# Masked attention with a residual on one core: the context matmuls of a pair of heads issued in one group instead of three

## The chip, the cores and the metric

The kernel runs on one core of a Trainium2 chip. A core has a matrix engine (TensorE, PE in the profile, with its weight loads as PEld), a vector engine (VectorE, DVE), an activation engine (ScalarE, ACT), a general engine (GpSimd, POOL) and an engine that issues transfers (SyncE, SP), all fed by instruction queues of their own and synchronised by semaphores. PE writes its results to PSUM; everything else lies in SBUF, 128 partitions wide both. The metric is the time of one execution on the device in microseconds.

## The reference

```python
def _L0_cond_ref(x, mask, Wq, Wo):          # x: (16, 512, 1024), mask: (16, 1024) of 0 and 1
    NH = 8
    B, D, T = x.shape
    dk = D // NH                            # 64
    scale = 1.0 / jnp.sqrt(dk)
    xt = jnp.transpose(x, (0, 2, 1))
    q = xt @ Wq.T
    qh = q.reshape(B, T, NH, dk).transpose(0, 2, 1, 3)
    scores = scale * jnp.einsum('bhqd,bhkd->bhqk', qh, qh)
    cmask = mask[:, None, None, :]
    rmask = mask[:, None, :, None]
    logits = (scores * cmask + (1.0 - cmask) * NEG) * rmask
    attn = jax.nn.softmax(logits, axis=-1)
    ctx = jnp.einsum('bhqk,bhkd->bhqd', attn, qh)
    ctx = ctx.transpose(0, 2, 1, 3).reshape(B, T, D)
    out = ctx @ Wo.T
    return jnp.transpose(out, (0, 2, 1))
x = x + _L0_cond_ref(x, cond_2048, L0_cond_Wq, L0_cond_Wo)
```

Queries, keys and values are one projection. A token whose mask is 0 is no key for the others, and its own row of logits is all zero, so its attention is the plain mean over all tokens.

## The kernel before

About half of the 1024 tokens of a batch element count. The kernel gathers those (up to C = 544 of them) into dense *slots*: four blocks of 128 slots and a *tail* of 32. Attention is computed among the slots alone. The others get the mean, which is projected once for a group of three or four batch elements and added to their rows.

The 16 batch elements go through a software pipeline. While element b has its scores and context computed, the next one, n = b + 1, has its rows transposed (`xt`, L398), projected to queries (`query`, L421) and transposed to values (`value`, L467), and the one before, o = b - 1, has its context normalised (`norm`, L664 to L670) and projected out (`project`, L680), added to the residual (L685) and scattered to the output (L764).

The attention of an element runs in 18 *steps*, the list `S` in `run`. A step is (p, i): pair of heads p (0 to 3) and slot block i (0 to 3); two more steps (p, None), after (0, 1) and after (2, 3), do the tails of four heads at once. In a step PE computes two score tiles (`scores`, L580: 4 matmuls of 128x272 for each head, in float16 with the low halves added by a second matmul), and ACT takes the exponential of each into a tile `p` of 128x544 in SBUF (L584), with the sums of the rows. The score tiles `pss` have two buffers. A tail step has 16 small matmuls (L555), one exponential (L559), a split into high and low parts on DVE (L564, L565) and four transfers by SP that spread them into `pt` (L571, L572).

The *context* of a pair is accumulated in one PSUM tile `pav`, which has one buffer. `attend(b, p, i, ps)` adds slot block i: 4 matmuls, L597, whose stationary operand is 128x64, so that the two heads of a pair write to partitions 0 to 63 and 64 to 127. They are in float32, and the profile counts each twice: 1024 in the program, 2048 in the trace. `attend(..., 4, None)` adds the tail with 4 matmuls of 128x128 (L600), and then ACT copies `pav` into an SBUF tile `c` (L604). `c` has three buffers, `p` has nine.

What `run` emits in a step, in order: the work that waits for this step (`free[st]`: sums of rows for the means, the reciprocals of the row sums in `recip_sums` and `recip_rows`, `norm`), the scores of both heads, one indirect transfer from the POOL queue (`issue`), and then a share of the *fill*, the list `m` of pieces of work for the elements n and o. Each piece has a cost in us, written out by hand, and the fill is dealt out so that after step st a share (st + 1) / 18 of the total has been emitted.

The context is emitted with the fill. `todo` gathers the `attend` calls of blocks 0 to 3 and `ready` holds those that are due. The blocks of steps 0 and 1 go out as one group in step 3, those of steps 2 and 3 as one group in step 1 of the next pair, and the tail, held in `whole`, goes out in step 2 of the next pair, between the scores of its two heads, with the copy of `pav` behind it:

```python
now = []
if i in (0, 2):
    ready, todo = todo, []
elif i in (1, 3):
    now, ready = ready, []
for f in fill + now if big else now + fill:
    f()
if i is not None:
    todo.append(L(self.attend, b, p, i, ps))
if i == 3:
    (whole if p < 3 else todo).append(L(self.attend, b, p, 4, None))
```

For the last pair of an element the tail goes with blocks 2 and 3, in step 1 of the next element.

The order emitted is not the order run. A list scheduler puts the instructions of all engines in order by their priority (the place where they were emitted, with an offset for some) and by when it holds their inputs and buffers to be ready, so it may put other work of PE into a group or split one.

The reciprocals of a pair: `recip_sums` (L619 to L627, DVE) two steps after its last block, `recip_rows` three steps after: a transpose on PE (L633, called *rr* here), a copy (L636), and SP transfers out to DRAM (L638) and back, broadcast (L641), for `norm`.

[...]

Of the kernel before, what the change touches and what calls it, by code (L numbers as in the profile page):

```python
# [10 lines left out]
F32 = mybir.dt.float32  # L11
# [8 lines left out]
P = 128  # L20
# [10 lines left out]
C = 544  # L31
CT = C - 512
CH = C // 2
# [16 lines left out]
class Fast:  # L50
# [491 lines left out]
    def scores(self, b, p, i):  # L542


        nc, s = self.nc, self.st[b]
        if "z" not in s:
            s["z"] = self.sb([P, H, 4], F32, "z", 2)
            s["zt"] = self.sb([P, 2], F32, "zt", 2)
        if i is None:
            pt = self.ps_s.tile([P, 2, 512], F32, tag="s", name="pss")  # L550
            for a in range(2):
                for g in range(2):
                    for r in range(HG):
                        xx, k = s["xx"][2 * p + r // 2], r % 2
                        self.beat = nc.tensor.matmul(pt[r * CT:(r + 1) * CT, g, :CH], lhsT=xx[:, 2 * k, 512:C],  # L555
                                                     rhs=xx[:, 2 * k + a, g * CH:(g + 1) * CH],
                                                     start=(a == 0), stop=(a == 1)).ins
            t = self.sb([P, C], F32, "p", 9)
            nc.scalar.activation(t.rearrange("p (g c) -> p g c", g=2), pt[:, :, :CH], AF.Exp,  # L559
                                 bias=s["nm"][p][:, HG:], scale=SCALE, accum_out=s["zt"][:, p:p + 1])  # L560

            hi = self.sb([P, C], F32R, "c", 3)
            lo = t.bitcast(F32R)
            nc.vector.tensor_copy(hi, t)  # L564
            nc.vector.tensor_tensor(lo, t, hi.bitcast(F32), ALU.subtract)  # L565

            def spread():
                s["pt"] = self.sb([P, 2, C], F32R, "pt")
                half = slice(0, DK), slice(DK, P)
                for k in range(2):  # L570
                    nc.sync.dma_start(out=s["pt"][half[k], k, :].bitcast(F32), in_=hi[half[k]].bitcast(F32))  # L571
                    nc.sync.dma_start(out=s["pt"][half[1 - k], k, :].bitcast(F32), in_=lo[half[k]].bitcast(F32))  # L572

            self.later(spread)
            return None
        xx, k = s["xx"][p // 2], p % 2
        pt = self.ps_s.tile([P, 2, 512], F32, tag="s", name="pss")
        for a in range(2):
            for g in range(2):
                self.beat = nc.tensor.matmul(pt[:, g, :CH], lhsT=xx[:, 2 * k, i * P:(i + 1) * P],  # L580
                                             rhs=xx[:, 2 * k + a, g * CH:(g + 1) * CH],
                                             start=(a == 0), stop=(a == 1)).ins
        t = self.sb([P, C], F32, "p", 9)
        self.exp = [nc.scalar.activation(t.rearrange("p (g c) -> p g c", g=2), pt[:, :, :CH], AF.Exp,  # L584
                                         bias=s["nm"][p // HG][:, p % HG:p % HG + 1], scale=SCALE,
                                         accum_out=s["z"][:, p, i:i + 1]).ins]
        return t

    def attend(self, b, p, i, ps):
        nc, s = self.nc, self.st[b]  # L590
        if i == 0:
            s["pav"] = self.ps_av.tile([P, 2, 512], F32, tag="av", name="pav")
        for g in range(2):
            for k in range(2):
                cols = slice(g * CH, (g + 1) * CH)
                if i < 4:
                    nc.tensor.matmul(s["pav"][k * DK:(k + 1) * DK, g, :CH], lhsT=s["v"][p][:, i, k * DK:(k + 1) * DK],  # L597
                                     rhs=ps[k][:, cols], start=(i == 0), stop=False)
                else:
                    nc.tensor.matmul(s["pav"][:, g, :CH], lhsT=s["vt"][p // 2][:, k, p % 2 * 2:p % 2 * 2 + 2, :],  # L600
                                     rhs=s["pt"][:, p % 2, cols], start=False, stop=(k == 1))
        if i == 4:
            c = self.sb([P, C], F32, "c", 3)
            nc.scalar.copy(c.rearrange("p (g c) -> p g c", g=2), s["pav"][:, :, :CH])  # L604
            s["c"].append(c)


    def recip(self, b, p):
# [191 lines left out]
    def run(self, flag):  # L800
        B = self.B
        L = lambda f, *a: lambda: f(*a)
        S = [(p, i) for p in range(NP) for i in range(4)]
        S.insert(2, (0, None))
        S.insert(13, (1, None))
        N = len(S)

        def xt(n):
            return [(0.45, L(self.xt, n, c)) for c in range(4)] + [(0.25, L(self.xt, n, 4))]

# [14 lines left out]
        for i, e in enumerate(ends):  # L825
            g = list(range(ends[i - 1] + 1 if i else 0, e + 1))
# [33 lines left out]
        def shift0():  # L860
            with self.tc.high_priority(offset=HPO):
                self.shift(0, 0)

        first = query(0, 0, 0) + xt(0)[3:] + [(0, L(self.facts, 0, 2))] + query(0, 1, 0) + query(0, 0, 1)
        first += [(0, index1)] + value(0, 0) + g1[:1] + query(0, 1, 1)[:1] + g1[1:2]
        first += [(0, L(self.split, "q", c, 1)) for c in range(DC)]
# [11 lines left out]
        begin += [(0, L(self.load, "o", c)) for c in range(DC)]  # L878
        begin += [(0, L(self.range_x, 0, c)) for c in range(DC)] + [(0, L(self.range_w, "q"))]
        groups = [(g, min(h, B)) for g, h in ((2, 4), (4, 8), (8, 12), (12, 16)) if g < B]  # L880
        todo, ready, whole = [], [], []
        for b in range(B + 1):
            o, n = b - 1, b + 1
            if b == B:
                self.last(o, todo)
                break
            free, early, late = {}, ([], []), []
            if b >= 1:
# [56 lines left out]
            total = sum(c for c, _ in m)  # L945
            done, pos = 0.0, 0
            for st, (p, i) in enumerate(S):
                soon, self.soon = self.soon, []
                for f in soon + free.get(st, []):
                    f()  # L950
                if i is None:
                    self.scores(b, p, None)
                else:
                    ps = [self.scores(b, 2 * p, i)]
                    if i == 2 and whole:
                        whole.pop()()
                    ps.append(self.scores(b, 2 * p + 1, i))

                for _ in range(1 if b < B - 2 else -(-len(self.urgent + self.spare) // (N - st))):
                    self.issue()  # L960
                goal = total * (st + 1) / N
                fill = []
                while pos < len(m) and (done + m[pos][0] / 2 <= goal or st == N - 1):
                    fill.append(m[pos])
                    done += m[pos][0]
                    pos += 1

                big = st >= 4 and [c >= 1 for c, _ in fill if c > 0.1][:1] == [True]
                fill = [f for _, f in fill]

                now = []
                if i in (0, 2):
                    ready, todo = todo, []
                elif i in (1, 3):
                    now, ready = ready, []
                for f in fill + now if big else now + fill:
                    f()
                if i is not None:
                    todo.append(L(self.attend, b, p, i, ps))
                if i == 3:  # L980
                    (whole if p < 3 else todo).append(L(self.attend, b, p, 4, None))
                    if p < 3:
                        free.setdefault(st + 2, []).append(L(self.recip_sums, b, p))
                        free.setdefault(st + 3, []).append(L(self.recip_rows, b, p))
                        if p < 2 or b == B - 1:
                            free.setdefault(st + 5, []).append(L(self.norm, b, p))
# [136 lines left out]


# [10 lines left out]
```

## Time and profile before

| | |
|---|---|
| four runs | 1133.4, 1133.7, 1134.68, 1137.15 us, median 1134.19 |
| the profiled execution | 1131.44 us, its span 1129.7 us |
| granted PE clock over it | 0.995 |
| ACT: exponentials L584 | 512, 363.3 us busy, 714 ns each |
| ACT: copy of the context L604 | 64, 38.7 us busy, 604 ns each |
| PE: scores L580 | 2048, 302.8 us busy |
| PE: context L597 and its tail L600 | 2048 and 256, 296.2 and 48.7 us busy |
| PE: queries L421 | 1536 of 128x272 or 128x274 |
| PE: output projection L680 | 852 in the program, of 128x512 for the most part |
| POOL: gathers and scatters L313, L764 | 284, about 1 us each |

Busy time is the union of an instruction group's records; matmuls are pipelined, so that each lasts longer than the distance to the next one. What a matmul costs is therefore read from the distances between starts, not from its length.

### The profile page before, as it was taken

How to read it: one execution, taken by the hardware profiler on the slowest of the kernel's cores; microseconds unless marked ns; L12 is line 12 of the kernel's file. 1: busy time of each engine (PE TensorE's matmuls, PEld its weight loads, DVE VectorE, ACT ScalarE, POOL GpSimd, SP SyncE). 2: the span in 40 equal slices, each digit the busy share in tenths (PEclk: the TensorE clock that was granted, in tenths of full speed). 3: DMA queues.
4: the chain of work that ended last, by engine and by line, in shares of the span. 5: the costliest groups of instructions: out<-in, count | busy, mean ns of one | idle time of the engine just before them, and what ended most of it. 6: DMA issues, size and time to landing. Idle time of an engine off the chain costs nothing.

```text
span 1129.7 us, 23296 instructions
## 1 busy us (share of the span) xinstructions
PE 1088.2 (96%) x8386; PEld 706.5 (63%) x8386; DVE 731.9 (65%) x2369; ACT 676.1 (60%) x1716; POOL 286.7 (25%) x303
## 2 busy tenths in 40 slices
PE   7899999999999999999999999999999999998997
PEld 6566666666666666566666666566666666665553
DVE  7687566765665667667665766856566665665643
ACT  5776665666566666566565665666656566654540
POOL 3001031322202222222222222232222222214542
PEclk9899999999999999999999999999999999999999
DMA  7745455645545464655655566455665654545652
GB/s 237 205 117 148 135 163 146 190 129 180 146 125 176 126 203 139 173 172 160 187 151 169 153 180 184 123 180 145 195 166 150 190 150 135 149 124 172 203 163 85
DMA packets 78122, 181.35 MB, mean 161 GB/s; under 512 B 15008, under 2 KB 16800, under 8 KB 78000
## 3 DMA queue, kind: packets, MB, share of 16 engines
q1 hardware_dynamic: 56816, 111.62, 36.0%
q0 software_dynamic: 21184, 68.18, 18.6%
q8 instruction: 68, 1.11, 0.4%
q14 instruction: 54, 0.44, 0.1%
HBM read 92.34 MB, written 33.91 MB: 112 GB/s over the span
## 4 chain that ended last, share of the span: by engine, by line
PE 68%; DVE 12%; DMA 9%; issue 6%; ACT 2%; POOL 2%; SPq 0%; DVEq 0%; POOLq 0%; ACTq 0%
PE pav L597 19%; PE pss L580 16%; PE pm L680 13%; PE pm L421 9%; PE pm L398 3%; DMA xi<-x_in,idx 2%; PE pav L600 2%; DMA rb<-rd 2%; PE pm L467 2%; POOL y_out L764 2%; DMA rd<-rr 1%; PE pm L633 1%; DVE c L664 1%; ACT p L584 1%; DMA xm<-x_nat_in 1%
## 5 line engine op out<-in xcount | busy, mean ns | idle before, releaser
L584 ACT ACTIVATE p<-pss,nm 128x544 f32<-128x544 f32 x512 | 363.3, 714 | 230.8 <-PE pss L580 219.3
L580 PE MATMUL pss<-xx 128*128 128x272 f16 x2048 | 302.8, 281 | 4.3 <-DMA xx<-hl 2.5
L597 PE MATMUL pav<-p,v 128*64 128x272 f32 x2048 | 296.2, 401 | 0.9 <-ACT c L604 0.9
L580 PEld LDWEIGHTS <-xx 128*128 128x128 f16 x2048 | 192.0, 99 | 85.4 <-issue 40.9
L597 PEld LDWEIGHTS pav<-p,v 128*64 128x64 f32 x2048 | 140.2, 136 | 104.6 <-issue 40.0
L764 POOL DMA_INDIRECT y_out<-xa,idx x68 | 68.3, 1005 | 304.1 <-PE pss L580 163.0
L421 PE MATMUL pm<-xh,wqh 128*128 128x274 f16 (+1 forms) x512 | 143.8, 281 | 0.1
L421 PE MATMUL pm<-xl,wqh 128*128 128x274 f16 (+1 forms) x512 | 143.3, 280 | 0.2 <-DVE xl L359 0.2
L421 PE MATMUL pm<-xh,wql 128*128 128x274 f16 (+1 forms) x512 | 143.4, 280 | 0.0
L313 POOL DMA_INDIRECT xa<-x_in,idx x68 | 70.3, 1034 | 182.4 <-PE pss L580 89.3
L421 PEld LDWEIGHTS <-wqh 128*128 128x128 f16 x1024 | 99.9, 99 | 22.0 <-issue 3.4
L584 ACT ACTIVATION_READ_ACCUMULATOR p<-pss,nm 128x1 f32 x512 | 102.7, 201 | 0.0
L685 DVE SCALAR_TENSOR_TENSOR xa<-pm,xa 128x512 f32<-128x512 f32 x60 | 41.3, 689 | 88.2 <-PE pm L680 88.1
L313 POOL DMA_INDIRECT xi<-x_in,idx x60 | 59.1, 986 | 152.9 <-PE pss L555 53.5
L680 PE MATMUL pm<-woh,ch 128*128 128x512 f16 x240 | 91.0, 379 | 0.5 <-DVE ch L667 0.5
L680 PE MATMUL pm<-woh,cl 128*128 128x512 f16 x240 | 91.0, 379 | 0.1
L680 PE MATMUL pm<-wol,ch 128*128 128x512 f16 x240 | 91.0, 379 | 0.0
L424 ACT ACTIVATE q<-pm 128x272 f32<-128x272 f32 (+1 forms) x128 | 51.0, 398 | 63.7 <-PE pm L421 63.5
L764 POOL DMA_INDIRECT y_out<-xi,idx x60 | 61.0, 1017 | 93.3 <-PE pss L580 73.5
L664 DVE TENSOR_TENSOR c<-c,rb 128x544 f32<-128x544 f32 x64 | 46.3, 723 | 48.6 <-DMA rb<-rd 40.4
L680 PEld LDWEIGHTS <-ch 128*128 128x128 f16 x480 | 46.0, 98 | 41.3 <-DVE ch L667 1.0
L751 DVE TENSOR_TENSOR xi<-xi,ub 128x512 f32<-128x512 f32 (+1 forms) x60 | 40.1, 688 | 42.1 <-DMA xi<-x_in,idx 29.5
(191 smaller groups left out, 1584.4 us busy)
## 6 DMA issues: line engine op xcount, KB each, us to landing
xx<-hl SPq DMA_DIRECT2D x256, 136.0 KB
xm<-x_nat_in SPq DMA_DIRECT2D x56, 512.0 KB
rb<-rd SPq DMA_DIRECT2D x128, 136.0 KB
pt<-c SPq DMA_DIRECT2D x64, 136.0 KB
pt<-p SPq DMA_DIRECT2D x64, 136.0 KB
ub<-ud SPq DMA_DIRECT2D x16, 256.0 KB
xi<-x_nat_in SPq DMA_DIRECT2D x8, 256.0 KB
xa<-x_in,idx POOLq DMA_INDIRECT x68, 4.1
```

The source lines that it names most:

```text
L313: dma = self.nc.gpsimd.indirect_dma_start(out=tile[:n], out_offset=None, in_=self.x, in_offset=bass.IndirectOffsetOnAxis(ap=idx, axis=0))
L398: self.pe = nc.tensor.transpose(pt[:, c, :], x[:n, c * P:(c + 1) * P], self.ident[:n, :n]).ins
L421: self.beat = nc.tensor.matmul(pq, lhsT=w[:, c, e * P:(e + 1) * P], rhs=xx[:, c, cols], start=(k == 0), stop=(k == 3 * DC - 1)).ins
L424: nc.scalar.activation(s["q"][:, e, cols], pq, AF.Copy, scale=1.0 / (SX * SW))
L580: self.beat = nc.tensor.matmul(pt[:, g, :CH], lhsT=xx[:, 2 * k, i * P:(i + 1) * P], rhs=xx[:, 2 * k + a, g * CH:(g + 1) * CH], start=(a == ...
L584: self.exp = [nc.scalar.activation(t.rearrange("p (g c) -> p g c", g=2), pt[:, :, :CH], AF.Exp, bias=s["nm"][p // HG][:, p % HG:p % HG + 1 ...
L597: nc.tensor.matmul(s["pav"][k * DK:(k + 1) * DK, g, :CH], lhsT=s["v"][p][:, i, k * DK:(k + 1) * DK], rhs=ps[k][:, cols], start=(i == 0), s ...
L664: nc.vector.tensor_tensor(c, c, s["rb"][p], ALU.mult)
L680: nc.tensor.matmul(po[:cols.stop - cols.start], lhsT=a[:, e, cols], rhs=w[:, e, :], start=(e == 0 and k == 0), stop=(e == DC - 1 and k == 2))
L685: self.nc.vector.scalar_tensor_tensor(x, po, 1.0 / (SX * SW), x, ALU.mult, ALU.add)
L751: self.nc.vector.tensor_tensor(x[:n], x[:n], s["ub"][:n], ALU.add)
L764: dma = self.nc.gpsimd.indirect_dma_start(out=self.out, out_offset=bass.IndirectOffsetOnAxis(ap=idx, axis=0), in_=x, in_offset=None)
```

## The change

- The context of a pair goes out as one group: blocks 0 to 3 are collected in `held` over the four steps of the pair, and with the tail behind them they make up `todo`, which is emitted in step 1 of the next pair, after that step's fill.
- The copy of `pav` to `c` leaves `attend` and becomes `keep`, emitted one step later, in step 2 of the next pair, after its fill. For the last pair of the last element it goes behind the group.
- The fill is no longer dealt evenly: `share` gives a step with a group 0.15 of a part, a tail step 0.7, the others 1.
- `p` has 14 buffers instead of 9, five times 544 x 4 bytes more in each partition.
- The pool for descriptors is set to 4096 bytes of each partition.

```diff
-            t = self.sb([P, C], F32, "p", 9)
+            t = self.sb([P, C], F32, "p", 14)
...
-        if i == 4:
-            c = self.sb([P, C], F32, "c", 3)
-            nc.scalar.copy(c.rearrange("p (g c) -> p g c", g=2), s["pav"][:, :, :CH])
-            s["c"].append(c)
+
+    def keep(self, b):
+
+        s = self.st[b]
+        c = self.sb([P, C], F32, "c", 3)
+        self.nc.scalar.copy(c.rearrange("p (g c) -> p g c", g=2), s["pav"][:, :, :CH])
+        s["c"].append(c)
...
+        share = [0.15 if i == 1 else 0.7 if i is None else 1.0 for _, i in S]
...
-        todo, ready, whole = [], [], []
+        todo, held, left, kept = [], [], [], []
...
-                self.last(o, todo)
+                self.last(o, todo + left)
...
-                    if i == 2 and whole:
-                        whole.pop()()
                     ps.append(self.scores(b, 2 * p + 1, i))
...
-                goal = total * (st + 1) / N
+                goal = total * sum(share[:st + 1]) / sum(share)
...
-                big = st >= 4 and [c >= 1 for c, _ in fill if c > 0.1][:1] == [True]
-                fill = [f for _, f in fill]
-
-                now = []
-                if i in (0, 2):
-                    ready, todo = todo, []
-                elif i in (1, 3):
-                    now, ready = ready, []
-                for f in fill + now if big else now + fill:
+                for _, f in fill:
                     f()
+
+                if i == 1:
+                    for f in todo:
+                        f()
+                    todo, kept = [], left
+                elif i == 2:
+                    for f in kept:
+                        f()
+                    kept = []
                 if i is not None:
-                    todo.append(L(self.attend, b, p, i, ps))
+                    held.append(L(self.attend, b, p, i, ps))
                 if i == 3:
-                    (whole if p < 3 else todo).append(L(self.attend, b, p, 4, None))
+                    todo, held = held + [L(self.attend, b, p, 4, None)], []
+                    left = [L(self.keep, b)]
...
-    nc = bacc.Bacc("TRN2", target_bir_lowering=False, num_devices=1)
+    nc = bacc.Bacc("TRN2", target_bir_lowering=False, num_devices=1, dynamic_dma_scratch_size=4096)
```

## The prediction

> **What bounds the kernel now.** First the page's head and PE's rows among the waits.
>
> ```profile
> span 1129.7 us, 23296 instructions
> PE 1088.2 (96%) x8386; PEld 706.5 (63%) x8386; DVE 731.9 (65%) x2369; ACT 676.1 (60%) x1716; POOL 286.7 (25%) x303
> ```
>
> ```profile
> PE pm L633 <- DVE rcol L627: 5.8, 5, 2.0
> PE pm L633 <- DVE m L511: 4.6, 6, 1.0
> PE pm L467 <- DVE q L427: 3.9, 5, 1.7
> PE pm L633 <- DVE rcol L624: 2.0, 3, 0.7
> PE pav L597 <- ACT c L604: 0.9, 3, 0.3
> PE pss L580 <- ACT p L559: 0.9, 2, 0.5
> PE pss L580 <- ACT p L584: 0.8, 2, 0.6
> ```
>
> (Engine and line, what it waited for: us in all, times, longest.) PE is busy 96% of the span and waits about 33 us in all its rows; no other engine is above 65%. So PE is the bound, and time is won by fewer PE cycles or fewer PE waits. The largest waits are those of the reciprocals' transpose, rr (L633): 5.8 + 4.6 + 2.0 = 12.4 us in 14 places.
>
> Busy time hides what PE loses inside its own stream. For that I read its timeline, distances between starts:
>
> ```profile
> 550.94 0.28 PE L421 MATMUL pm<-xl,wqh 128*128 128x272 f16 x1
> 551.06 0.28 PE L421 MATMUL pm<-xh,wql 128*128 128x272 f16 x1
> 551.27 2.05 PE L597 MATMUL pav<-p,v 128*64 128x272 f32 x16
> 553.25 0.65 PE L555 MATMUL pss<-xx 128*32 128x272 f16 x16
> 553.83 0.29 PE L421 MATMUL pm<-xh,wqh 128*128 128x274 f16 x1
> ```
>
> ```profile
> 62.52 0.67 PE L597 MATMUL pav<-p,v 128*64 128x272 f32 x2
> 63.12 0.64 PE L580 MATMUL pss<-xx 128*128 128x272 f16 x4
> ...
> 509.75 0.68 PE L597 MATMUL pav<-p,v 128*64 128x272 f32 x4
> 510.36 0.33 PE L633 MATMUL pm<-ident,rcol 128*128 128x128 f32 x1
> ```
>
> A full-width matmul starts 0.115 us after the one before, but the first 64-column one starts 0.21 after its predecessor: 0.095 for entering. The run of 16 records (8 matmuls, 4 pairs of heads) takes 1.98 us until the next kind, that of 4 records (one pair) 0.61, and that of 2 records (one head alone) 0.60. So a pair costs (1.98 - 0.61) / 3 = 0.457 us, a head alone as much as a pair, and a run has 0.61 - 0.457 = 0.153 on top. **A run of context matmuls costs 0.095 + 0.153 = 0.25 us over its work**, however long it is.
>
> **The change, part by part.** I count in the order in which the built programs issue their matmuls, not in the source, since other work gets into a group.
>
> *Runs.* Before, the 1024 context matmuls stand in 198 runs (88 of the intended 8), afterwards in 162. Only 23 groups come out whole, as 16 in a row; the others are cut by transposes of rows, values and reciprocals. 36 x 0.25 = 9.0 us less. Heads cut from their partner: 552 pair times before, 554 after, 2 x 0.457 = 0.9 more. The 32-column runs of the tail steps go from 45 to 41; the one shown takes 0.58 us for 16 records that go four at a time, 4 x 0.115 = 0.46, so 0.12 on top, and entering costs about 0.1 as above: 4 x 0.2 = 0.8 less.
>
> *Tails.* The tail (L600) stood behind scores in 48 of 64 cases, behind the context in 16; now in all 64.
>
> ```profile
> 532.47 0.63 PE L580 MATMUL pss<-xx 128*128 128x272 f16 x4
> 532.85 0.77 PE L600 MATMUL pav<-pt,vt 128*128 128x272 f32 x4
> 533.46 1.16 PE L580 MATMUL pss<-xx 128*128 128x272 f16 x8
> ...
> 512.13 0.77 PE L600 MATMUL pav<-pt,vt 128*128 128x272 f32 x4
> 512.74 0.49 PE L398 MATMUL pm<-ident,xa 128*128 128x128 f32 x3
> ```
>
> Behind scores it starts 0.03 after the last of them (532.47 + 3 x 0.116 = 532.82), so it costs 0.03 + 0.61 - 0.116 = 0.52; behind a context run, whose leaving is priced already, 0.61. 48 x 0.09 = 4.3 us more. PE's own stream: -9.0 + 0.9 - 0.8 + 4.3 = **-4.6 us**.
>
> *Waits of rr.* Before, 13 of the 64 rr stand directly behind the value transposes, and in 11 of these it waits, for some 8 of the 12.4 us: 0.45 us of transposes is all that PE has to do while DVE finishes. In the new order 57 stand behind context or tail matmuls, with up to 4.4 us of PE work (16 matmuls 4 x 2 x 0.457 = 3.7, entering and fixed part 0.25, tail 0.6) in which DVE makes the reciprocals; 4 stand behind values. I keep 4/13 of the 12.4 us: -8.6. Bounds: all of it gone, -12.4; none, 0.
>
> *The fill, dealt unevenly.* The parts sum to 4 x 0.15 + 2 x 0.7 + 12 = 14.0 instead of 18. An element takes about 66 us (1050 us of the span for 16). A step with a group now has 0.93 (eight score matmuls of 0.116) + 4.4 + a little fill, about 5.6 us, a tail step some 2, which leaves (66 - 22 - 4) / 12 = 3.3 us to a plain step, before 66 / 18 = 3.7. In that, DVE has its fill: 732 / 16 = 45.7 us an element, less 15.5 for norms and reciprocals that go by step (2.59 + 1.28 us for a pair, sums of their rows), over 14: 2.2 us; where a norm falls 4.8, and it is 1.5 behind for a step. New waits follow where PE needs such an output soon: L467 on the query's copy and mask. They are bounded by nothing below and by the 20 us of PE's other waits above. I take the nearest row, L467 <- L427 (3.9 us, with 0.3 for ACT), and let it double: +4.2.
>
> *The copy, a step later.* 0.60 us on ACT (L604), whose wait PE sees for 0.9 us now. It lies behind the exponentials of two heads and before the next group by two steps, some 6 us: I cost it at nothing for PE; if that cover goes it is 64 x 0.60 = 38 us. `c` is needed by `norm` five steps after the pair, two after the copy. For an element's last pair the norm follows a step after the copy, and the projection of the element before stands right behind: DVE's 2.6 us there have 12 query matmuls and 16 scores, 3.3 us, as cover. [...]
>
> *Fourteen `p` tiles.* A pair and half the next take 12, a tail step one more; the 15th is asked for behind the group that frees the first. Nothing.
>
> *The smaller pool of descriptors.* No row shows a wait for room. The queue's 284 transfers take, by the medians from issue to landing (4.1, 3.2, 4.0, 4.0, 3.3, 3.1, 5.0 us by kind), 1079 us if one had to land before the next: even then the queue gets through the span, and gathers are issued an element ahead; the last five scatters would then end 4 x 3.2 + 5.0 - 8 = 10 us later (8 us is what now lies between PE's end at 1121.7 and the span's). Between 0 and 10 I take 0. [...]
>
> **Sum:** -4.6 - 8.6 + 4.2 = -9.0 us on the profiled execution's 1131.44 (span 1129.7 and 1.7 around it): 1122.4. The median shown is 2.75 above that execution, so **1125 us**.
>
> **The rivals.**
> 1. *Given back.* The denser steps make 10 to 16 us of new waits instead of 4. For: norms put DVE 1.5 us behind once in a pair. Against: each is followed by a group in which DVE has little. -4.6 - 8.6 + 13 = 0: 1134.
> 2. *ACT becomes the bound behind the group, slower.* Place: the plain steps after a group. ACT has two exponentials, 0.70 apart in its timeline, 1.4; its other work is 247 us of rows, 15.4 an element, 1.1 a part: 2.5 of 3.3 us. With the copy (0.6) in front, or a row sum (L343, 1.06), it is at or over 3.3, and the scores have two buffers only. From 0.26 us lost for a pair ((13.2 + 3.4) / 64) this decides; half the copy exposed is 19.2 - 13.2 = +6.0, 1140; all of it 1159. Against: PE waited 1.7 us for exponentials in the whole run, ACT 219 us for scores, and it idles 3 us in each group.
> 3. *The change does what it says in full:* 64 runs, no head alone: -134 x 0.25 - 40 x 0.457, some 50 us, 1085. The built order rules it out but for the chance that I misread it.
> 4. *The pool blocks* gathers or the last scatters: 10 us less gain, 1135.
>
> **Chances.** Forecast 0.64; given back, with the pool, 0.16; ACT 0.18; in full 0.02. What a measurement of this kernel can tell from no change is about 0.3%, 3.4 us. Faster than 1130.8: 0.64 + 0.02 = 0.66; within: 0.16; slower than 1137.6: 0.18. Range: with all of rr's waits gone and none new -17.0, 1117, and two below for the execution's spread; up into the second rival to its half, 1140: **1115 to 1140**; the forecast alone 1117 to 1131.
>
> **What would show it.** In the profile after: runs of 32 records of L597 in 3.9 us including the entry, followed by L600 0.6 long; rr's waits under 5 us; L467's about 8; the sum of PE's waits 28 instead of 33; ACT's copy at 604 ns and no PE row for it over 2 us; POOL's transfers still 1.0 us each. It is wrong if PE's waits for exponentials (L580 <- L584) grow to over 10 us, if new waits of PE exceed 13 us, or if transfers of POOL lengthen.

## The result, and the profile after

The changed kernel takes 1136.98 us (median of 52 runs, 1130.02 to 1144.74), the kernel before 1134.55 (78 runs, 1128.35 to 1140.21). The ratio is 1.0021, 95% interval 1.0012 to 1.0030: 2.4 us slower, where 9.0 less were forecast. The profiled execution took 1143.35 us, near the top of these runs, while that of before (1131.44) lies below its median. So the two spans differ by 11.5 us, and only some 2.4 of it belong to the change. Some 6 us is PE's clock in just these two executions: the granted mean was 0.995 before and 0.990 after, and 1141.2 x 0.010 - 1129.7 x 0.005 = 5.8 us is an estimate of what that cost. Over all its recorded runs the changed kernel has 0.993, the kernel before, in the runs beside the experiments, 0.991 to 0.992: as far as the record goes, the clock is not what makes the medians differ.

The page's head of the changed kernel, and PE's largest rows among its waits (engine and line, what it waited for: us in all, times, longest):

```profile
span 1141.2 us, 23203 instructions
PE 1089.2 (95%) x8386; PEld 718.8 (63%) x8386; DVE 729.9 (64%) x2369; ACT 671.0 (59%) x1716; POOL 298.7 (26%) x303
```

```profile
PE pm L636 <- DVE rcol L630: 8.2, 10, 2.2
PE pm L509 <- DVE smcol L507: 5.2, 5, 3.3
PE pm L467 <- DVE nm L520: 4.9, 8, 1.1
PE pm L467 <- DVE q L427: 4.6, 5, 1.5
...
PE pm L421 <- DVE tmp L487: 2.2, 3, 1.1
PE pm L484 <- DVE rcol L630: 2.2, 4, 1.3
PE pss L580 <- ACT p L584: 1.3, 2, 0.9
```

(The code has three lines more from L603 on: rr's transpose, L633 before, is L636, its copy L639, `norm` L667 to L673, the projection's addition L688.) All rows of PE together make 42.0 us, those that end on DVE 33.5. Before they made 32.6 and 25.2, and in a second profile of the same order (experiment e1) 35.4, so 34.0 on the mean. **PE waits 8 us more, and it is DVE that it waits for.** (That is one profile. Those of e5, e7 and e9 below, whose orders are close to the changed one, have 40.4, 39.5 and 37.2, so 3 to 8 us more is what can be said.) rr's waits are still 8.7 us. New are L509, which had none, L484 behind the same `rcol`, and 2.2 us of L421; L467 has 10.1 instead of 4.5. No row is left of PE waiting for the copy of `pav`, and the exponentials have 1.3 us.

PE's own work did get shorter, as it should. Of L597 by lines, busy us after the bar (296.2 before):

```profile
L597 PE MATMUL pav<-p,v 128*64 128x272 f32 x2048 | 291.1, 402 | 0.0
```

And in its timeline a group that came out whole, with the tail and a third row behind it that doesn't wait (start, length, what, records):

```profile
532.35 3.89 PE L597 MATMUL pav<-p,v 128*64 128x272 f32 x32
536.16 0.77 PE L600 MATMUL pav<-pt,vt 128*128 128x272 f32 x4
536.77 0.27 PE L636 MATMUL pm<-ident,rcol 128*128 128x128 f32 x1
```

### The profile page after: what moved, and what is told of

Same layout as the page of the kernel before. It is cut to its first block, busy times and chain, and to the rows that moved or that the text cites. A ratio compares the mean times of both kernels' runs of the same rounds, so it can differ in the third digit from the quotient of the medians.

```text
span 1141.2 us, 23203 instructions
## 1 busy us (share of the span) xinstructions
PE 1089.2 (95%) x8386; PEld 718.8 (63%) x8386; DVE 729.9 (64%) x2369; ACT 671.0 (59%) x1716; POOL 298.7 (26%) x303
## 4 chain that ended last, share of the span: by engine, by line
PE 59%; DVE 18%; DMA 14%; issue 5%; ACT 2%; SPq 1%; POOL 1%; DVEq 0%; POOLq 0%
PE pav L597 18%; PE pss L580 12%; PE pm L683 12%; PE pm L421 7%; DMA rb<-rd 7%; DMA rd<-rr 4%; PE pav L600 3%; PE pm L398 3%; DMA xi<-x_in,idx 2%; DVE c L667 2%; DVE p L565 1%; DVE hl L436 1%; PE pm L467 1%; DVE tmp L458 1%; PE pm L636 1%
## 5 line engine op out<-in xcount | busy, mean ns | idle before, releaser
L597 PE MATMUL pav<-p,v 128*64 128x272 f32 x2048 | 291.1, 402 | 0.0
L580 PEld LDWEIGHTS <-xx 128*128 128x128 f16 x2048 | 196.4, 99 | 70.7 <-issue 26.5
L597 PEld LDWEIGHTS pav<-p,v 128*64 128x64 f32 x2048 | 144.3, 137 | 96.9 <-issue 26.3
L421 PE MATMUL pm<-xh,wqh 128*128 128x274 f16 (+1 forms) x512 | 143.5, 280 | 3.1 <-DVE tmp L487 2.2
L421 PE MATMUL pm<-xh,wql 128*128 128x274 f16 (+1 forms) x512 | 143.3, 280 | 0.0
L421 PE MATMUL pm<-xl,wqh 128*128 128x274 f16 (+1 forms) x512 | 143.2, 280 | 0.0
L607 ACT COPY c<-pav 128x544 f32<-128x544 f32 x64 | 39.1, 610 | 162.1 <-PE pav L600 158.6
L421 PEld LDWEIGHTS <-wqh 128*128 128x128 f16 x1024 | 100.4, 99 | 25.6 <-issue 6.8
L313 POOL DMA_INDIRECT xa<-x_in,idx x68 | 73.3, 1077 | 163.7 <-PE pss L580 69.3
L313 POOL DMA_INDIRECT xi<-x_in,idx x60 | 63.5, 1059 | 163.5 <-PE pss L555 52.4
L639 DVE COPY rr<-pm 10x128 f32<-10x128 f32 x64 | 17.8, 278 | 95.6 <-PE pm L636 94.4
L688 DVE SCALAR_TENSOR_TENSOR xa<-pm,xa 128x512 f32<-128x512 f32 x60 | 41.2, 687 | 53.7 <-PE pm L683 53.6
```

What stands on the lines that cost most here:

```text
L313: dma = self.nc.gpsimd.indirect_dma_start(out=tile[:n], out_offset=None, in_=self.x, in_offset=bass.IndirectOffsetOnAxis(ap=idx, axis=0))
L421: self.beat = nc.tensor.matmul(pq, lhsT=w[:, c, e * P:(e + 1) * P], rhs=xx[:, c, cols], start=(k == 0), stop=(k == 3 * DC - 1)).ins
L607: self.nc.scalar.copy(c.rearrange("p (g c) -> p g c", g=2), s["pav"][:, :, :CH])
L688: self.nc.vector.scalar_tensor_tensor(x, po, 1.0 / (SX * SW), x, ALU.mult, ALU.add)
```

## Where rr waits, and why

A wait's row gives a line, but a line runs 64 times. Put in order of time, the rr of pairs 0, 1 and 3 never wait, neither before nor after: **all of rr's waits, in both kernels, are at the third pair of an element.** Its reciprocals come right behind the tail step that makes two of its row sums. This is one such place in the changed kernel, DVE's timeline (the bracket is idle time before it) and then PE's:

```profile
492.32 0.73 DVE L667 TENSOR_TENSOR c<-c,rb 128x544 f32<-128x544 f32 x1 [0.29 <-DMA rb<-rd]
...
494.49 0.43 DVE L564 CAST c<-p 128x544 fp32r<-128x544 f32 x1
...
495.54 0.71 DVE L565 TENSOR_TENSOR p<-p,c 128x544 fp32r<-128x544 f32 x1
...
497.03 0.36 DVE L627 TENSOR_TENSOR rcol<-zt,corr 32x1 f32<-32x1 f32 x2
...
498.43 0.68 DVE L459 TENSOR_REDUCE sd<-tmp 128x8 f32<-128x512 f32 x1
499.02 0.16 DVE L630 TENSOR_TENSOR rcol<-rcol,hit 128x10 f32<-128x10 f32 x1
```

```profile
496.70 2.05 PE L597 MATMUL pav<-p,v 128*64 128x272 f32 x14
499.33 0.30 PE L636 MATMUL pm<-ident,rcol 128*128 128x128 f32 x1 [0.59 <-DVE rcol L630]
```

From 492.3 to 499.2 DVE works without a gap: a `norm`, the split of the tail's exponentials (L564, L565), a split of queries, squares of values, and the five reciprocal instructions threaded between. And the third pair's rr does not stand behind the group, but inside it, after 14 of its 32 records in 10 of the 16 elements (directly behind value transposes in four more). Its cover is 2.05 us of PE, not 4.4. The ten wait 0.48 to 2.16 us each, 8.2 in all; the four behind value transposes wait only 0.14 each.

## The experiments

In all of them the kernel before ran on the same chip beside them, and the ratios are to it. The table gives for each kernel what PE's *stream*, its own work without waits, should gain by the prices of the prediction (runs and pair times counted in the built order, with its terms for tails and 32-column runs), the sum of PE's waits in its profile, what both make together (stream + waits - 34.0), and what was measured (ratio - 1, times 1134.5).

| kernel | runs / pairs | stream, us | PE waits, us | together | measured, us | ratio, interval |
|---|---|---|---|---|---|---|
| before / e1 | 198 / 552 | 0 | 32.6 / 35.4 | 0 | -1.1 (e1) | 0.9990 (0.9974 to 1.0006) |
| changed | 162 / 554 | -4.6 | 42.0 | +3.4 | +2.4 | 1.0021 (1.0012 to 1.0030) |
| e5 | 162 / 554 | -4.6 | 40.4 | +1.8 | +3.3 | 1.0029 (1.0010 to 1.0048) |
| e6 | 149 / 545 | -12.2 | 34.8 | -11.4 | -8.8 | 0.9922 (0.9891 to 0.9952) |
| e7 | 168 / 558 | -1.0 | 39.5 | +4.5 | +4.5 | 1.0040 (1.0020 to 1.0061) |
| e9 | 160 / 554 | -5.4 | 37.2 | -2.2 | +1.6 | 1.0014 (0.9992 to 1.0035) |
| e10 | 195 / 552 | -0.9 | 32.0 | -2.9 | -1.9 | 0.9983 (0.9969 to 0.9998) |
| e12 | 146 / 543 | -13.9 | 56.1 | +8.2 | +17.4 | 1.0153 (1.0132 to 1.0175) |
| e13 | 163 / 555 | -4.3 | 32.6 | -5.7 | -5.2 | 0.9954 (0.9934 to 0.9974) |
| e14 | 162 / 554 | -4.6 | 37.4 | -1.2 | -5.2 | 0.9954 (0.9926 to 0.9981) |
| e15 | 163 / 555 | -4.3 | 31.1 | -7.2 | -6.0 | 0.9947 (0.9927 to 0.9967) |
| e16 | 149 / 545 | -12.2 | 31.8 | -14.4 | -18.3 | 0.9839 (0.9812 to 0.9866) |
| e17 | 191 / 551 | -3.2 | 23.7 | -13.5 | -14.3 | 0.9874 (0.9856 to 0.9893) |
| e18 | 195 / 552 | -0.8 | 32.7 | -2.1 | -6.5 | 0.9943 (0.9928 to 0.9958) |
| e2 | 64 / 512 | -46.9 | 72.6 | -8.3 | +26.1 | 1.0230 (1.0189 to 1.0271) |
| e8 | 135 / 535 | -21.2 | 64.9 | +9.7 | +22.3 | 1.0197 (1.0162 to 1.0232) |
| e11 | 125 / 535 | -23.3 | 58.4 | +1.1 | +16.9 | 1.0149 (1.0126 to 1.0172) |

Down to e18, but for e12, the two columns agree within 5 us. That is the account as far as the table can tell, for 5 us is more than the change itself, and the waits are from one profile each: two profiles of the same order, before and e1, differ by 2.8. For e12 and the three last the columns leave 9 to 34 us out. Part of this is, by an estimate, PE's clock. With spans of the profiled executions instead of medians, and (1 - granted clock) x span as an estimate of the clock's cost, what stream, waits and clock leave out is 5 us for e12 (span 25.0 over that of before), and 21, 11 and 9 us for e2, e8 and e11 (32.5, 28.2 and 20.1 over).

**e1. The pool alone.** The kernel before with the smaller pool of descriptors and nothing else:

```diff
-    nc = bacc.Bacc("TRN2", target_bir_lowering=False, num_devices=1)
+    nc = bacc.Bacc("TRN2", target_bir_lowering=False, num_devices=1, dynamic_dma_scratch_size=4096)
```

> The kernel before with the descriptor pool of 4096 bytes and nothing else; every engine's order is that of before. Theory 1 (the change is even because PE's stream got about 5 us shorter and PE waits for DVE about 9 us longer): the pool does nothing, ratio 1.000 within 0.002, mean of L313 and L764 at 0.99 to 1.03 us as before. Theory 2 (the smaller pool slows GpSimd's transfers and costs the gain): 3 to 8 us slower, ratio 1.003 to 1.007, L313 at 1.06 to 1.08 us as in the profile after.

1137.05 us, the kernel before beside it 1137.32. The pool does nothing that can be measured, as forecast.

**e2. The groups whole.** The changed kernel, with every group kept together behind the step's last score matmul and raised in priority:

```diff
                 if i == 1:
-                    for f in todo:
-                        f()
+                    with self.behind(self.beat), self.tc.high_priority(offset=HPO):
+                        for f in todo:
+                            f()
```

> The changed kernel with each group issued behind the last score or query matmul of its step and at high priority, so that all 64 groups stay whole (64 runs instead of 162, 512 pair times instead of 554). Theory 1 with the price of 0.25 us a run and 0.457 us a pair: PE's stream 42 us shorter than in the changed kernel; even if its waits grow by 10 to 15 us, 1105 to 1112 us, ratio to before 0.973 to 0.98. Rival (a run's fixed cost isn't saved by joining runs, the price is wrong): PE's stream stays, 1135 to 1150 us, ratio 1.00 to 1.015.

1161.98 us, 26 us slower than before. The price of runs held: L597's busy time is 46.9 us under that of before (the bracketing prices are 134 x 0.153 + 40 x 0.457 = 38.8 inside the runs, 51.8 with their entries). PE's waits and L597, by waits and by lines:

```profile
PE pm L421 <- DVE nm L520: 11.6, 5, 2.8
PE pss L580 <- ACT p L584: 9.0, 14, 1.3
PE pm L467 <- DVE q L427: 8.1, 10, 1.5
PE pm L484 <- DVE xa L688: 5.9, 5, 2.1
```

```profile
L597 PE MATMUL pav<-p,v 128*64 128x272 f32 x2048 | 249.3, 396 | 0.1
```

So the third rival of the prediction, all groups whole, is no gain at all: PE's waits are 72.6 us, against 42.0 in the changed kernel. That a PE which runs ahead in lumps of 4.4 us has to wait for the other engines in between is read from these rows, not shown by a run of its own.

**e3 and e4. Less work for DVE.** The kernel before (e3) and the changed one (e4) without the 64 reductions of L366 and the 16 behind them, some 47 us of DVE work that nothing else needs but the flag of the range:

```diff
-        nc.vector.tensor_reduce(s["top4"][:, c:c + 1], self.xh[:, c, :CM + 1], AX.X, ALU.max, apply_absolute_value=True)
-        if c == DC - 1:
-            nc.vector.tensor_reduce(self.big[:, b:b + 1], s["top4"], AX.X, ALU.max)
+        if b == 0 and c == 0:
+            nc.vector.memset(self.big, 0.0)
```

> The kernel before without the check of the range of x (64 reductions of 706 ns on DVE, L366, and 16 small ones; the maxima are set to zero instead), 47 us of DVE work less. Theory 1 (PE waits on a late DVE, more so in the changed kernel): the waits of the reciprocals' transpose fall by a third to a half, 3 to 6 us faster, ratio 0.995 to 0.997. Rival 3 (the waits come from the order on PE and ACT, not from DVE's load): within 0.2%.

> The changed kernel without the check of the range of x, 47 us of DVE work less. Theory 1: PE's waits on DVE (33 of 42 us) fall by a third to a half, 8 to 14 us faster than the changed kernel, 1123 to 1129 us, ratio to before 0.99 to 0.995, and so now 3 us or more faster than the kernel before with the same cut. Rival 3: as much as the kernel before gains from the same cut, still 2 us slower than it.

Ratios 0.9983 (0.9966 to 0.9999) and 1.0000 (0.9980 to 1.0020): 1.9 and 2.4 us less than the kernels they come from, about a twentieth of the work removed, and as much in the one as in the other. Even this may be the clock: its mean over these runs was 0.994 in both, 0.991 in the kernel before beside them, some 3 us by the estimate above. PE's waits are 36.4 and 42.8 us, no less than with the reductions. DVE's load isn't what the change ran into; what counts is when single results are there (e13 to e15).

**e5. Reciprocals earlier, at the wrong pairs.**

```diff
-                        free.setdefault(st + 2, []).append(L(self.recip_sums, b, p))
+                        free.setdefault(st + (1 if p < 2 else 2), []).append(L(self.recip_sums, b, p))
```

> The changed kernel, with the reciprocals of the first and second pair of an element (recip_sums, DVE) emitted one step earlier; PE's order is nearly the same (162 runs, 554 pairs as in the changed kernel), so PE's own stream stays. Theory A (PE waits for DVE's results because DVE stands in order behind the group and its results are late; 10.9 us of the waits are those of rr and what it holds up): with half of the reciprocals a step earlier, half of these waits go, 4 to 6 us less than the changed kernel, ratio to the kernel before about 0.997 to 0.998. Theory B (what is not waited for here is waited for at the next place, since DVE as a whole is late): same as the changed kernel, ratio 1.001 to 1.004, rr's waits smaller but others larger by as much.

1135.75 us, 1133.24 before: nothing. It looks like a vote for theory B, but it only moved the first and second pair, whose rr never wait, so it tells nothing of either.

**e6. rr's copy on ACT.**

```diff
-            nc.vector.tensor_copy(rr, pt[:10])
+            nc.scalar.copy(rr, pt[:10])
```

> The changed kernel, with the copy of rr out of PSUM (L639) on ACT instead of DVE, so that DVE doesn't stand idle behind it until the group has ended (94.4 us in the changed kernel, 35.0 before). The built order has 149 runs and 545 pair times, 12.2 us less of PE's stream than the kernel before, 7.6 less than the changed one. Theory A (DVE's standing behind rr is what makes its results late): the stream's 7.6 us come, and PE's waits for DVE fall by 5 or more: 1122 to 1128, ratio 0.990 to 0.994. Theory B (any gain of the stream comes back as waits): ratio 0.999 to 1.004. Rival C (ACT is the one short of time behind the group: exponentials stand behind rr's copy): PE's waits for exponentials (L580 for L584) grow from 1.3 to over 8 us, ratio over 1.004.

1125.66 us: 11 us under the changed kernel. Theory A's number, but not its reason. DVE's order around the third pair is nearly the same as above. What differs is PE's, at the same element:

```profile
489.90 2.51 PE L597 MATMUL pav<-p,v 128*64 128x272 f32 x18
492.52 0.30 PE L636 MATMUL pm<-ident,rcol 128*128 128x128 f32 x1
```

With another engine for the copy the scheduler put 18 records in front of the third rr instead of 14, 0.46 us more of PE, and the wait of 0.59 is gone; in the whole run rr has no row left. With the shorter stream that is the gain: by the table 7.6 of stream and 7.2 of waits against the changed kernel, 11.2 measured.

**e7. The copy of `pav` at once**, in the group's own step:

```diff
                     for f in todo:
                         f()
-                    todo, kept = [], left
-                elif i == 2:
-                    for f in kept:
-                        f()
-                    kept = []
+                    for f in left:
+                        f()
+                    todo, left = [], []
```

> The changed kernel without 'a step behind': the copy of pav (keep) is emitted directly behind its group, in the same step. The built order has 168 runs and 558 pair times: by the prices of a run and a pair 1.0 us less than the kernel before, 3.6 more than the changed one. Theory A: ACT stands behind L600 in both, so this part costs what the stream says: about 1139 to 1141, ratio 1.003 to 1.007. If the later copy was the harm (context waits for the copy, ACT's order): faster than the changed kernel, ratio under 1.000. If the later copy is what keeps ACT off the scores' path: PE's waits for exponentials grow by over 5 us, ratio over 1.008.

1137.99 us, 1133.24 before: 2 us behind the changed kernel, where the stream says 3.6; the two intervals overlap. "A step behind" is worth its few runs and has no part in the loss.

**e8 and e11. Groups kept whole without raised priority**, with rr's copy on DVE (e8) and on ACT (e11): the edit of e2 without `high_priority`, and for e11 that of e6 with it. In the order that ran, 41 of the 64 groups are whole in either, against 64 in e2 and 23 in the changed kernel.

> The changed kernel with the group kept behind the step's last score matmul, but without raised priority: 135 runs, 535 pair times, 21.2 us less of PE's stream than the kernel before by the prices (with raised priority it was 46 less and 60 to 80 us of waits and half clock more). Theory A: more blocks stand whole, so DVE and ACT stand longer behind them: excess over the stream of 85 to 100 us instead of 71, 1135 to 1145, ratio 0.999 to 1.008. If wholeness itself is harmless and only the raised priority did harm in that kernel: the stream's gain comes, 1118 to 1124, ratio under 0.991.

> The kernel with the group kept behind the step's last score matmul (without raised priority) and the copy of rr on ACT: 125 runs, 535 pair times, 23.3 us less of PE's stream than the kernel before, 11.1 less than with the copy on ACT alone. Theory A in its strong form (rr's copy is what made whole groups dear): 1113 to 1120, ratio 0.982 to 0.988. If the other in-order waits (the projection's evacuation L688, ACT's exponentials behind the copy of pav) are enough: excess of 85 us or more instead of 61, 1135 to 1150, ratio 1.000 to 1.015.

1156.69 and 1150.93 us. The loss stays without raised priority, and with rr's copy on ACT as well, so neither of them alone is the harm. PE's waits are 64.9 and 58.4 us, with the projection's addition (L484 for L688, 14.0 and 12.8 us) and the exponentials (9.5 and 9.4) in front.

**e9. rr's copy on DVE without its raised priority.**

```diff
-            with self.tc.high_priority(offset=HPO):
-                nc.vector.tensor_copy(rr, pt[:10])
+            nc.vector.tensor_copy(rr, pt[:10])
```

> The changed kernel, with the copy of rr (L639) still on DVE but without its raised priority, so that other DVE work that is ready goes ahead of it. The built order has 160 runs and 554 pair times: PE's stream as in the changed kernel, within 1 us. Theory A (DVE's standing behind rr during the group costs PE's waits afterwards): DVE's wait at L639 falls from 94 to under 50 us, PE's waits for DVE fall, 3 to 8 us less than the changed kernel: ratio to the kernel before 0.994 to 0.999. Theory B (what the copy on ACT won was its shorter stream alone): no change from the changed kernel, ratio 1.001 to 1.004. Rival D (the transpose's pm buffer is what counts, and it is held longer now): PE's waits for pm grow, ratio over 1.005.

1133.69 us, 1133.64 before. It didn't do what it was for: DVE stood 94.7 us at the copy, as with the priority (94.4). Inconclusive.

**e10. rr's copy on ACT in the kernel before**, the edit of e6.

> The kernel before (two groups, tail apart) with the copy of rr on ACT. 195 runs, 552 pair times: 0.9 us less of PE's stream. Theory A: DVE stood behind rr for 35.0 us only, in 41 places, so there is little to win: ratio 0.997 to 1.001; the copy on ACT pays only with the long group. Theory E (the copy on ACT is a gain by itself, whatever the groups): 5 us or more as in the changed kernel, ratio under 0.996, and then the grouping is still worth only its stream.

1132.05 us, 1133.64 before. The copy on ACT by itself wins 2 us; there rr keeps its waits (12.9 us in all, 2.0 of them at one fourth pair). This fits e6's reading: not the engine of the copy, but the place of rr.

**e12. The first two pairs' reciprocals and rr a step earlier**, on top of e6 (the edit of e5, and `recip_rows` at `st + 2` for them).

> The copy of rr on ACT, and recip_sums and recip_rows of the first and second pair a step earlier: 146 runs, 543 pair times, 1.7 us less of PE's stream than with the copy on ACT alone. With recip_sums alone a step earlier the changed kernel won nothing, so theory A expects the stream only: ratio 0.989 to 0.993. If the waits of L484 for rcol (4.0 us with the copy on ACT) go as well: ratio 0.985 to 0.989.

1154.11 us, 1133.64 before: by the ratios 26 us slower than e6, with nearly the same stream. Now pairs 0 and 1, which never waited, do:

```profile
PE pm L636 <- DVE rcol L630: 15.7, 19, 2.2
```

Some 12 of these 15.7 us are at pairs 0 and 1, where PE had paid nothing.

**e13 to e15. The tight places, one at a time and together.** With PE's stream unchanged: the third pair's `recip_rows` a step later (e13), the first value transposes of an element behind the next query piece (e14), both (e15).

```diff
-                        free.setdefault(st + 3, []).append(L(self.recip_rows, b, p))
+                        free.setdefault(st + (4 if p == 2 else 3), []).append(L(self.recip_rows, b, p))
```

```diff
-                m = xt(n)[:1] + early[0] + xt(n)[1:2] + chunk2 + xt(n)[2:3] + early[1] + xt(n)[3:] + tp + query(n, 0, 0) + query(n, 0, 1) + bt + value(n, 0)
-                m += query(n, 1, 0) + late + P_(0) + query(n, 1, 1) + P_(1)
+                m = xt(n)[:1] + early[0] + xt(n)[1:2] + chunk2 + xt(n)[2:3] + early[1] + xt(n)[3:] + tp + query(n, 0, 0) + query(n, 0, 1) + bt
+                m += query(n, 1, 0) + value(n, 0) + late + P_(0) + query(n, 1, 1) + P_(1)
```

> The changed kernel with recip_rows of the third pair alone a step later (all of rr's waits, in the kernel before and in the changed one, are at the third pair, whose reciprocals come right behind a tail step). 163 runs, 555 pair times: PE's stream as in the changed kernel, 0.3 us more. Theory F (the new waits stand at a few places where the order by hand leaves DVE too little time, above all the third pair's rr and the first value transposes): rr's waits fall from 8.2 us, with 2.2 for L484 behind rcol, to under 2, and the kernel gains 6 to 10 us on the changed one: ratio to the kernel before 0.993 to 0.997. Theory B (DVE as a whole is late, and what isn't waited for here is waited for at the next place): rr's waits go, others grow by as much, ratio 1.000 to 1.004.

> The changed kernel with the first value transposes of an element (value(n, 0), L467) behind the next query piece instead of in front of it. 162 runs, 554 pair times, exactly those of the changed kernel. Theory F: L467's waits (4.9 for nm L520 and 4.6 for q L427) fall from 9.5 us to under 3 and the kernel gains 5 to 8 us on the changed one: ratio 0.995 to 0.998. Theory B: other waits grow by as much, ratio 1.000 to 1.004.

> The changed kernel with both: the third pair's recip_rows a step later and the first value transposes behind the next query piece. 163 runs, 555 pair times. Theory F: both gains add, 11 to 17 us, and the forecast of the change comes out after all: ratio 0.987 to 0.993. Theory B: ratio 0.999 to 1.004.

1130.31, 1130.59 and 1128.63 us, 1133.91 before: 7.6, 7.6 and 8.4 us less than the changed kernel. So single places, as theory F has it, though the two don't add up. In e14 part of the wait only changes its line: L421 now waits 3.9 us for the same nm L520. And some 3 us of e14's gain may be the clock, whose mean was 0.994 in its runs and 0.991 in the kernel before beside them. And e13 settles theory A. DVE's wait at rr's copy in the changed kernel, then in e13:

```profile
DVE rr L639 <- PE pm L636: 94.4, 49, 4.9
```

```profile
DVE rr L639 <- PE pm L636: 126.9, 55, 4.9
```

DVE stands there 32 us longer, and the kernel is 7.6 us faster. That an engine stands idle in order behind a group cost nothing here by itself.

**e16. The best of it**: e6 and e14 together.

> The copy of rr on ACT (0.992 by itself, its rr waits are gone already), and the first value transposes behind the next query piece: 149 runs, 545 pair times, as with the copy on ACT alone. Theory F: L467's waits (6.0 and 4.4) go, 6 to 10 us less: ratio 0.983 to 0.987. Theory B: ratio 0.990 to 0.994.

1117.74 us, 1133.91 before: 0.9839 (0.9812 to 0.9866), the fastest of all, 16 to 18 us under the kernel before (by the medians and by the ratio).

**e17 and e18. The same edits in the kernel before.** e17 has those of e15, e18 those of e16.

> The kernel before (two groups) with both moves: the third pair's recip_rows a step later and the first value transposes behind the next query piece. 191 runs, 551 pair times, 3.2 us less of PE's stream. The kernel before has rr's waits at the same place (12.2 us, all at the third pair) and 3.9 us of L467. If the places are tight whatever the grouping: 8 to 14 us less, ratio 0.988 to 0.993, and the grouping is worth its stream alone. If they became tight by the grouping: the stream and a little, ratio 0.995 to 0.999.

> The kernel before with the two edits of the best kernel so far (copy of rr on ACT, first value transposes later), without the grouping: 195 runs, 552 pair times, 0.8 us less of PE's stream. With the copy on ACT alone it stood at 0.998, its rr waits still 10.9 us. If the grouping is what makes these edits pay: ratio 0.996 to 1.000. If they pay by themselves: under 0.993.

1122.29 and 1130.89 us, 1137.01 before. e17 answers the question of its expectation: the third rr was a tight place all along, and with it and the value transposes moved the kernel *without* the grouping gains 14 us; rr's waits fall from 12.4 to 1.6. (The rr was not moved alone in the kernel before.) PE's waits of e17, then of e15:

```profile
PE pm L467 <- DVE q L427: 2.6, 2, 1.9
PE pm L421 <- DVE nm L520: 2.2, 1, 2.2
...
PE pm L509 <- DVE xl L359: 1.0, 2, 0.7
```

```profile
PE pm L421 <- DVE nm L520: 6.2, 10, 1.8
PE pm L509 <- DVE smcol L507: 5.2, 5, 3.3
```

With the same two places eased, the grouped kernel still waits 7.4 us more (31.1 against 23.7), on `top` (L509) and on what stands behind `bottom` (L520), the two pieces that make `nm`, the bound which the exponentials subtract. Its ratio is 0.0073 higher (0.9947 against 0.9874), 8 us, with a stream only 1.1 us shorter. e16 and e18 show the other side: where the built order has 149 runs instead of 195 and waits are equal (31.8 and 32.7), grouping is worth 0.0104, 11.8 us, and the stream's difference is 11.4. Between them lies the same pair without the move of the values, e6 and e10: 6.9 us gained, with 2.8 us more of waits and 11.3 less of stream. Each of these differences is good to 3 or 4 us. **Grouping is worth its runs, less what it does to the places where DVE has just enough time.**

## Why the prediction failed, step by step

- *What bounds the kernel*: right. PE is at 95%, and stream plus waits give the time within 5 us wherever the groups aren't forced whole, e12 apart.
- *Runs, pairs, tails, -4.6*: right as far as it can be seen. L597's busy time fell by 5.1; the prices give 36 x 0.153 - 0.9 = 4.6 for what lies inside the runs. e16 against e18 (11.4 us by the prices, 11.8 measured, good to some 3 us) agrees with the price of a run by time.
- *Waits of rr, -8.6*: **the step that failed first.** 12.4 became 8.7, not 3.8. I had sorted the 64 rr by what stands before them, found most of the waits behind the value transposes, kept the share of the four that stay there, and took up to 4.4 us of a group as cover for the other 57. But the waits belong to one rr of an element, the third pair's. Of these, nine that left the value transposes, and the last element's, stand after 14 records of a group, with 2.05 us of cover and 7 us of DVE work ahead in the one looked at, and these ten wait 8.2 us; the four that stayed, for which I had kept 3.8, wait 0.14 each. Which rr stands where in a group was never looked at; the trace of before, in order of time, already shows that the waits are all at the third pair.
- *New waits, +4.2*: **the second.** I looked for them at L467 alone and let its row double. It came to 10.1 - 4.5 = 5.6; L509 (5.2), L484 behind rr's `rcol` (2.2) and L421 (2.2) came on top, 15.2 in all (L398 gave 2.1 back), more than the 13 us which the prediction named as a sign of being wrong. L509 had no row before and so no price.
- Together the two steps said -4.4 for waits, and 42.0 - 34.0 = +8.0 came in the one profile: 12.4 us more, about the whole distance from the forecast -9.0 to the measured +2.4.
- *The copy a step later, nothing*: right; no row of PE waits for it (before, 0.9 us), and e7 puts it at no cost.
- *`p` tiles and pool, nothing*: right for the pool (e1). The gathers (L313, the 128 of `xa` and `xi`) did lengthen, from 1034 and 986 ns to 1077 and 1059, but with the pool alone they take 1024 and 994, so it isn't the pool alone; PE waits for a gather once, at the start, 2.9 us against 1.5. The prediction had named longer transfers as a sign of being wrong. The `p` tiles were not tried apart.
- *The rivals*: the first, "given back" (10 to 16 us of new waits, 1134), came nearest: 15.2 us of new waits. But it still had rr's -8.6, which didn't come, and the norm which it names as a cause is seen in front of the third rr; whether it stands in front of the new waits too was not looked at. ACT as the bound did not show: exponentials 1.3 us. The third, in full, would not have been 1085 but, built with raised priority, 1162 (e2). That the time lies inside 1115 to 1140 is luck: the upper part of that range was there for ACT.

Open: why kernels with whole groups, and e12, lose 5 to 21 us beyond stream, listed waits and clock; and why the three kernels with the values moved alone (e14, e16, e18) are some 4 us faster than stream and waits say. That `top` and `bottom` get tight because a step with a group has little fill to part them is read from the traces, and no run moved them. No run kept the group and dealt the fill evenly, so how much of the new waits comes from the dealing, as the prediction had it, and how much from the group isn't shown.

## What to carry to other kernels

Before a wait's row is priced, sort its instances by the loop's index: 14 waits of one line may be one place in 16 rounds, and then it is moved by one line of code, which here, with one other piece moved, was worth 14 us without any regrouping of the matmuls (e17). When PE's work is gathered into longer lumps, price what PE asks for right behind the lump and inside it, by how much work its producer has in its queue at that place, not by the producer's load: here 47 us less of DVE's work was worth 2.4 us at most (e4), two pieces moved 8.4 (e15). An engine's long idle row is no cost until someone is shown to wait for it: in e13 DVE stood 32 us longer, and the kernel took 7.6 us less.

## What the runs showed of the hardware

In the changed kernel's trace PE's clock went to half after each of two waits, of 3.31 us for `smcol` (until 1045.50), and of 2.16 us for the last element's third rr (until 1106.88). Windows around both (from and to, length, busy us of PE, PEld, DVE, ACT and POOL, granted clock, DMA share, GB/s):

```profile
1043.26:1046.67 3.41, 1.17 (x7) 0.72 (x7) 1.04 (x4) 0.37 (x1) 2.80 (x3) 1.00 1.02 279
1046.60:1053.60 7.00, 6.52 (x28) 3.60 (x27) 2.71 (x7) 1.52 (x4) 0.09 (x1) 0.51 0.38 139
```

```profile
1104.70:1108.11 3.41, 1.25 (x12) 0.77 (x12) 2.22 (x12) 0.00 (x0) 0.00 (x0) 1.00 0.85 240
1108.00:1111.40 3.40, 3.40 (x18) 2.00 (x15) 0.00 (x0) 0.61 (x1) 0.00 (x0) 0.52 0.24 80
1111.40:1116.00 4.60, 4.60 (x31) 2.68 (x31) 1.41 (x4) 2.39 (x7) 0.97 (x1) 0.99 0.17 64
```

The granted clock is 0.50 from 1046.67 to 1053.50 and from 1108.11 to 1111.52, which cost an estimated 3.4 and 1.7 us (half of each) on top of the waits where PE has work. Not every wait of some 2 us was followed by this. In the kernel before, PE waits 2.03 us for rr (until 1095.65), and the clock stays at 1.00:

```profile
1091.60:1095.01 3.41, 2.02 (x14) 0.92 (x13) 3.25 (x13) 2.21 (x6) 2.37 (x3) 1.00 0.40 142
1095.01:1098.43 3.42, 2.78 (x21) 1.67 (x21) 0.80 (x4) 0.80 (x2) 0.96 (x1) 1.00 0.89 257
```

In the two windows of 3.41 us that end where the clock halves, PE stood 2.24 and 2.16 us; the wait of the kernel before falls on two such windows with 1.39 and 0.64. In both traces, of the kernel before and of the changed one, the changes of the clock lie whole multiples of 3.413 us apart (in the changed kernel, 6.827 us at half from 1046.67 on, then 54.613 at full, 3.413 at half, 27.307 at full). Cut at such multiples into lengths of 3.413 us, the two have 612 at full clock between us 60 and 1112. The two in which PE stood 2.24 and 2.16 us are the only ones of these with a length at half behind them; the next longest, 1.57 us (before, 1033.61 to 1037.02), was followed by full clock. This is what the two traces have; no run was made to try it.

The mean granted clock of the profiles lies between 0.995 (before) and 0.979 (e2, where PE's waits make 72.6 us). By the estimate under the table the clock makes some 19 us of what e2 lost; no run tried it apart.
